# A two-layer graph transformer on one core: the lookups of layer 1's late neighbours done in one run ahead of the edge stage's products, weights moved to SP's queue, last table pieces over fewer slots, and another order of riding chunks

## The chip, the cores and the metric

The kernel runs on one core of a Trainium2 chip. The metric is the device time of one execution in microseconds, the median of several runs. A core has five engines that run at the same time, each with its own stream of instructions: TensorE (PE, matmuls), VectorE (DVE), ScalarE (ACT), GpSimd (POOL) and SyncE (SP). ACT, POOL and SP also issue DMA transfers, each through a queue of its own.

## What is computed

There are 6250 nodes with 128 features, 100000 edges sorted by destination, 16 node types, 32 edge types and 8 heads of 16. One layer of the reference, with the node types' matrices picked by type:

```python
k = typed_linear(x, ntype, Wk); q = typed_linear(x, ntype, Wq); v = typed_linear(x, ntype, Wv)
kT = einsum('nhd,htdo->nhto', k, Watt)          # every node for every edge type
vT = einsum('nhd,htdo->nhto', v, Wmsg)
a = einsum('ehd,ehd->eh', kT[src, :, etype], q[dst]) * pri[:, etype].T / SQRT_D
msg = vT[src, :, etype] * edge_softmax(a, dst)[:, :, None]
hag = segment_sum(msg, dst)
h = silu(typed_linear(hag, ntype, Wa))
h = h * alpha + x * (1 - alpha)                  # alpha = sigmoid(skip[ntype])
x = layernorm(h) * g + b
```

Two such layers follow each other, then `h @ ff_w + ff_b`, and the result is layernorm(input + that).

## The kernel before

**Table and gathers.** Each layer has a table in device memory with one row of 1 KB (K and V, 256 floats) for each pair of a node and an edge type. A put (L1085 in layer 0, L1915 in layer 1, both POOL) writes the rows of 128 nodes for 16 of the edge types, 2 MB; a layer has 98 puts. Destinations are sorted by their number of edges and laid out in blocks of 128, one to a partition, three or four blocks to a superblock. For each edge slot of a block POOL gathers 128 rows of the table with one instruction (L1691, `kv<-tab,ell`) into one column of a ring of 50 columns (`SLOTS`); `ell` holds the row numbers.

**Stages.** First the preparation and layer 0's table: PE, ACT and DVE make the rows, and a ranking of the nodes runs beside it on DVE (`rank_order`). Then `edges()` goes through "visits": fourteen superblocks of layer 0, two "early" visits of layer 1, then layer 1's fourteen. A visit's blocks each take: the products of gathered K with the query (L1707), their reductions (L1712), and a generator `finished()` that makes the softmax (exponentials on ACT at L1492 and L1502), V times weight (L1518), its sums (L1529, L1534). The steps of one block's `finished()` are taken between the products of the next; a ring column is free again when its L1518 is done. After the last block of a superblock `nodes()` makes the new node rows (L1741 `rd`, L1748 `hag`, the typed matrix, the layernorm), and in layer 0 `table()` makes from them the superblock's part of layer 1's table (`kvT` L1870, PE L316, copies into one of three `st` buffers at L323 on ACT and L321 on DVE, put at L1915).

**Pace.** Generators for queries, node rows and table pieces are advanced by `tick`, so many steps for each edge slot (`spread(of, gen, steps, slots)`). POOL's instructions keep the order in which the program writes them. On the other engines a list scheduler sets the order when the kernel is built.

**Lookups.** The two early visits of layer 1 may only read rows of the table that are written early. Their 32 + 44 gathers use lists `ells`, in which slots with late sources are sorted behind. To know which sources are late, `looked()` splits node numbers into row and column, transposes them, writes them to `looks` in device memory (L1282) and reads them back spread over all partitions (L1302), compares them (L1326, `is_equal`), multiplies with a table of late nodes on PE (L1328), compares again (L1333), and turns the flags back with 86 small matmuls and 42 ACT copies (L1319). Its scratch is the third part of `wkqv`, so layer 1's `Wq` is loaded there only afterwards. A sort (tile `key`, MAX and MATCH_REPLACE) then makes `ells` and `negs`. The whole is one generator of 27 steps over 62 slots (`LOOK`), and `table()` runs what is left of the lookups before layer 1's first piece (`while not done`).

**Weights.** Layer 1's `Wk`, `Wv` and its edge weights (`load_edge_weights`, for each head `bdk`, `bdv`, `prit`, L245 to L248) are issued on ACT's queue at the start of the edge stage, ahead of visit 0's query.

**Riders.** In some blocks the last slots are filled in only a few partitions. Such slots "ride" in spare lanes of another slot's gather and are copied into place by SP (L1687, `kv<-kv`). A block with riders is cut into a lead chunk, a bundle with the riders, and a rest.

## Time and profile before

| | before |
|---|---|
| median of 3 runs | 2951.08 us (2948.94 to 2956.63) |
| profiled execution | 2950.59 us, span 2948.7 us |
| granted TensorE clock, mean | 0.652 |
| POOL | 1983.6 us busy (67%), 2118 instructions |
| DVE | 1828.0 us (62%), 4117 |
| PE | 1778.6 us (60%), 5415 |
| ACT | 1108.4 us (38%), 2580 |
| first gather of layer 0 | at 605.2 us |
| first put of layer 1's table | at 752.2 us |
| first gather of layer 1's rest | at 1938.2 us |

A row of a timeline has the start, the duration, the engine, the source line, the operation and what it writes and reads; brackets hold the idle time of the engine just before and what ended it. An engine name with a q (SPq, ACTq) is an issue of a DMA. A row of windows has, after the window and its length, busy time and count for PE, PEld, DVE, ACT and POOL, the granted clock, the DMA engines' share and GB/s. A row of groups has line, engine, operation, tiles, count, busy time, mean time of one in ns, and the idle time before them by releaser.

### The profile page before, as it was taken

What the parts mean: (1) busy time and instruction counts of PE and PEld (TensorE: products, weight loads), DVE (VectorE), ACT (ScalarE), POOL (GpSimd) and SP (SyncE); (2) the same over time, 40 slices, a digit from 0 to 9 for tenths busy, and PEclk for the clock granted to TensorE, in tenths of its full rate; (3) what the DMA queues carried; (4) which work ended last, traced back from release to release, by engine and by line L of the source; (5) the groups of instructions that cost most, each with busy time, mean ns of one, the idle gap of its engine ahead of it and who ended that gap; (6) DMA issues with size and microseconds to landing.
All of it is one profiled execution on the core that took longest, in us unless ns stands there. A gap on an engine that the chain in (4) does not pass through costs nothing. (4 is left out here: it accounts for less than half of the span.)

```text
span 2948.7 us, 22842 instructions
## 1 busy us (share of the span) xinstructions
PE 1778.6 (60%) x5415; PEld 763.8 (26%) x5415; DVE 1828.0 (62%) x4117; ACT 1108.4 (38%) x2580; POOL 1983.6 (67%) x2118
## 2 busy tenths in 40 slices
PE   5999999724676888887587887701433323313121
PEld 2445444411222243232133222200211212101010
DVE  8358323228866777666586655746887767666663
ACT  4876655501423423344243455412332222222220
POOL 5323665566677677777777765767777767777776
PEclk9979766655766656567577566555656656655555
DMA  7998999986667767787787888873333323333331
GB/s 230 403 395 358 385 399 406 396 223 183 217 214 270 272 228 239 266 302 252 257 297 246 287 331 327 306 223 104 105 106 104 107 86 105 106 105 105 106 101 51
DMA packets 186105, 678.28 MB, mean 230 GB/s; under 512 B 55586, under 2 KB 101328, under 8 KB 160912
## 3 DMA queue, kind: packets, MB, share of 16 engines
q0 software_dynamic: 113248, 636.05, 60.8%
q1 hardware_dynamic: 56852, 34.57, 4.3%
q10 hardware_dynamic: 15856, 6.06, 1.0%
q8 instruction: 46, 0.75, 0.1%
q14 instruction: 103, 0.84, 0.1%
HBM read 254.44 MB, written 421.89 MB: 229 GB/s over the span
## 5 line engine op out<-in xcount | busy, mean ns | idle before, releaser
L1691 POOL DMA_INDIRECT kv<-tab,ell x1454 | 1389.2, 955 | 508.5 <-issue 372.6
L323 ACT COPY st<-tb 128x512 f32<-128x512 f32 (+1 forms) x1052 | 717.1, 754 | 540.4 <-PE tb L316 356.2
L1707 DVE TENSOR_TENSOR kv<-kv,tb 128x768 f32<-128x768 f32 (+6 forms) x278 | 262.0, 946 | 534.2 <-DMA kv<-tab,ell 352.8
L292 PE MATMUL nb<-xm,weights 128*128 128x384 f32 (+2 forms) x640 | 368.9, 728 | 351.1 <-DVE xm L275 349.6
L316 PE MATMUL tb<-bdv,kvT 32*128 32x512 f32 x784 | 305.5, 935 | 102.7 <-ACT st L323 99.8
L316 PE MATMUL tb<-bdk,kvT 32*128 32x512 f32 x784 | 294.4, 941 | 35.7 <-ACT st L323 27.7
L316 PE MATMUL tb<-bdv,vT 32*128 32x512 f32 x784 | 290.4, 821 | 33.3 <-ACT st L323 27.5
L292 PEld LDWEIGHTS nb<-xm,weights 128*128 128x128 f32 x640 | 158.8, 269 | 570.9 <-DVE xm L275 359.7
L1712 DVE TENSOR_REDUCE a<-kv 128x48 f32<-128x768 f32 (+6 forms) x278 | 260.0, 939 | 0.7
L1085 POOL DMA_INDIRECT tab<-st,rows x98 | 101.2, 1033 | 199.0 <-ACT st L323 163.0
L1529 DVE TENSOR_TENSOR tb<-kv,tb 128x512 f32<-128x512 f32 (+6 forms) x412 | 228.1, 554 | 2.5
L316 PE MATMUL tb<-bdk,kT 32*128 32x512 f32 x784 | 221.3, 835 | 1.2 <-DVE st L321 0.6
L321 DVE COPY st<-tb 128x512 f32<-128x512 f32 (+1 forms) x124 | 94.1, 759 | 189.7 <-PE tb L316 111.8
L1691 POOL DMA_INDIRECT kv<-tab,ells x166 | 158.9, 957 | 66.9 <-issue 45.9
L1518 DVE TENSOR_TENSOR kv<-kv,tb 128x768 f32<-128x768 f32 (+10 forms) x258 | 192.3, 763 | 0.8
L300 PE MATMUL nb<-ident,hag 128*128 128x128 f32 x98 | 25.9, 406 | 275.5 <-DVE hag L1748 275.5
L275 DVE SCALAR_TENSOR_TENSOR xm<-ntb,nb 128x512 f32<-128x512 bf16 (+2 forms) x224 | 126.7, 593 | 48.1 <-PE nb L300 39.3
L1492 ACT ACTIVATE tb<-a,m 128x17 f32<-128x17 f32 (+12 forms) x328 | 95.3, 290 | 161.9 <-DVE m L1485 153.4
L316 PEld LDWEIGHTS tb<-bdv,vT 32*128 32x128 f32 x784 | 115.0, 230 | 129.8 <-ACT st L323 104.0
L316 PEld LDWEIGHTS tb<-bdv,kvT 32*128 32x128 f32 x784 | 83.5, 255 | 244.4 <-ACT st L323 199.5
L1915 POOL DMA_INDIRECT tab<-st,row x98 | 100.8, 1029 | 67.1 <-ACT st L323 32.7
L316 PEld LDWEIGHTS tb<-bdk,kvT 32*128 32x128 f32 x784 | 80.6, 257 | 181.8 <-ACT st L323 133.9
(395 smaller groups left out, 2274.3 us busy)
## 6 DMA issues: line engine op xcount, KB each, us to landing
kv<-tab,ell POOLq DMA_INDIRECT x1454
weights<-looks SPq DMA_DIRECT2D x40, 128.0 KB
hr<-xrd SPq DMA_DIRECT2D x16, 256.0 KB
kv<-tab,ells POOLq DMA_INDIRECT x166
xrd<-xr POOLq DMA_DIRECT2D x10, 256.0 KB
weights<-looks SPq DMA_DIRECT2D x40, 64.0 KB
hrd<-hs SPq DMA_DIRECT2D x8, 256.0 KB
hr<-xrd SPq DMA_DIRECT2D x10, 192.0 KB
```

The source lines that it names most:

```text
L275: nc.vector.scalar_tensor_tensor(xm[:, :n], ntb[:, :n], float(t), hT[:, :n], op0=ALU.is_equal, op1=ALU.mult)
L292: nc.tensor.matmul(ps[:, :n], w[:, t, :], xm[:, :n], start=(t == types[0]), stop=(t == types[-1]))
L316: nc.tensor.matmul(pt[:, b], yT[s, i * P:(i + 1) * P], bd[s, tt, :], start=True, stop=True)
L323: nc.scalar.copy(to, pt)
L1085: put = nc.gpsimd.indirect_dma_start(out=tabs[0].rearrange("(n t) c -> n (t c)", t=16), out_offset=bass.IndirectOffsetOnAxis(ap=rows1[:, t ...
L1492: nc.scalar.activation(w[:, :, h], av[:, :, h], AF.Exp, scale=-1.0, bias=m[:, h:h + 1], accum_out=den[:, i, h:h + 1])
L1518: nc.vector.tensor_tensor((v_[:, k0:k1] if j or k0 else acc[:, :k1]) .rearrange("p k (h d) -> p k h d", h=H), v_[:, k0:k1].rearrange("p k ...
L1529: nc.vector.tensor_tensor(to, v_, to, op=ALU.add)
L1691: get = nc.gpsimd.indirect_dma_start(out=to.bitcast(I32) if l else to, out_offset=None, in_=tabs[l][:], in_offset=bass.IndirectOffsetOnAxi ...
L1707: nc.vector.tensor_tensor(kk, kk, q[:lanes].unsqueeze(1).to_broadcast([lanes, c, D]), op=ALU.mult)
L1712: nc.vector.tensor_reduce(a[:lanes, j0:j1, :], kk.rearrange("p k (h d) -> p k h d", h=H), axis=AX.X, op=ALU.add)
L1915: put = nc.gpsimd.indirect_dma_start(out=tabs[1].rearrange("(n t) c -> n (t c)", t=16), out_offset=bass.IndirectOffsetOnAxis(ap=row2[:, tg ...
```

## The change

Six things are changed. The lines of the changed kernel are 4 to 70 higher (L1691 becomes L1749, L1707 L1770, L1518 L1576, L1915 L1983, L323 L327).

1. Splitting, transposing and writing the node numbers to `looks` moves into `rank_order`, so into the preparation.
2. `lookups()` replaces the first part of `looked()`. It is run as a whole between the third step of visit 0's query and the rest of it. Loads come in six groups of up to four steps into the three `st` buffers, 128x4x1024 in one transfer; one comparison covers 128x1024; the flags of all 22 steps are summed in one PSUM bank of 44 rows by matmuls with shifted columns of `rowsum`, then copied once (ACT, 44x512), transposed four times and copied to `flags` in four pieces.
3. Layer 1's `Wk`, `Wv`, `Wq` and the 24 loads of edge weights are issued on SP, behind the lookups' loads.
4. The sort is a generator of its own, one step every 11 slots (`SORT`); the wait for the lookups in `table()` is gone.
5. The pieces of layer 0's last visit are spread over 0.62 of the slots in place of 1.0.
6. A bundle with riders is brought into the ring in its old place, but multiplied after the other chunks, and its chunks come last in `finished()` as well.

```diff
-LOOK = 62.0
+SORT = 11.0
+DEEP = 4
...
-    def load_typed(to, w):
-        nc.scalar.dma_start(to, w.rearrange("t d o -> d t o"))
+    def load_typed(to, w, queue=nc.scalar):
+        queue.dma_start(to, w.rearrange("t d o -> d t o"))
...
+                def load(g):
+                    if g >= len(groups):
+                        return
+                    e, n0_, n1_ = groups[g]
+                    st = ep.tile([P, 16, 2 * D], F32, name="st", bufs=STB)
...
+                            nc.sync.dma_start(to, of.unsqueeze(0).to_broadcast(list(to.shape)))
...
+                for g in range(STB):
+                    load(g)
+                sums_ps, turn_ = pairs[0][:R, 0], 0
+                for g, (e, n0_, n1_) in enumerate(groups):
+                    for n in range(n0_, n1_):
...
+                            nc.vector.tensor_scalar(now[:, :2], now[:, :2], rowk, None,
+                                                    op0=ALU.is_equal)
...
+                                nc.tensor.matmul(pt[HALF * h:HALF * (h + 1), :w[h]],
+                                                 lates[:, e, :], now[:, h, :w[h]],
+                                                 start=True, stop=True)
...
+                            nc.vector.scalar_tensor_tensor(
+                                now[:r, 3, a:b], now[:r, 2, a:b], halves[:r],
+                                pt[:r, a:b], op0=ALU.is_equal, op1=ALU.mult)
...
+                            nc.tensor.matmul(sums_ps[:, a:b], rowsum[:r, at:at + R],
+                                             now[:r, 3, a:b], start=(e == n == 0), stop=final)
+                        yield
+                    load(g + STB)
...
-            for _ in queries0(got.setdefault(0, []), *visits[0][1]):
+            asking = queries0(got.setdefault(0, []), *visits[0][1])
+            for _ in range(3):
+                next(asking)
+            for _ in lookups():
+                pass
+            for i, w in enumerate((Wk, Wv, Wq)):
+                load_typed(wkqv[:, i], w[1], nc.sync)
+            load_edge_weights(1, queue=nc.sync)
+            for _ in asking:
                 pass
...
-            done = []
-            spread(extra, looked(), 27, LOOK)
+            spread(extra, sorted_slots(), 1.0, SORT)
...
-                    while not done:
-                        next(extra[0][0])
                     tables[v] = gen
                     spread(pieces, gen, 8 * visits[v][1][1] + 4,
-                           (1.0 if v + 4 < n0 else 0.5 if v + 2 < n0 else 1.0) *
+                           (1.0 if v + 4 < n0 else 0.5 if v + 2 < n0 else
+                            1.0 if v + 1 < n0 else 0.62) *
                            slots(min(v + 2, first1 - 1)))
...
-                    for bundle in bundles:
-                        for (j0, j1, lanes), kv in zip(bundle, [bring(*c[:2]) for c in bundle]):
+                    later = [b for b in bundles[:-1] if riding and len(b) > 1]
+                    for bundle in bundles + later:
+                        if id(bundle) not in brought:
+                            brought[id(bundle)] = [bring(*c[:2]) for c in bundle]
+                            if any(bundle is b for b in later):
+                                continue
+                        for (j0, j1, lanes), kv in zip(bundle, brought[id(bundle)]):
...
-                for i, w in enumerate((Wk, Wv) if fast else (Wk, Wv, Wq)):
-                    load_typed(wkqv[:, i], w[1])
-                load_edge_weights(1)
                 if fast:
                     edges()
                     break
```

How the change moves instructions is seen at three places. The first is SP's queue at the start of the edge stage, in the changed kernel; `ntb` and `hr` are the node types and rows that a visit's query and `nodes()` need, the first pair is visit 0's, the pair at the end visit 1's.

```order
L1179 DMA ntb<-typed 128x384
L1187 DMA hr<-xrd 128x3x128
L1318 DMA st<-looks 128x4x1024
L1318 DMA st<-looks 64x4x512 x2
...
L240 DMA weights<-in_L_gnn_Wq_dram 128x16x128
L249 DMA bdk<-in_L_gnn_Watt_dram 16x32x16
L250 DMA bdv<-in_L_gnn_Wmsg_dram 16x32x16
L252 DMA prit<-in_L_gnn_pri_dram 16x32
...
L1179 DMA ntb<-typed 128x384
L1187 DMA hr<-xrd 128x3x128
```

Before, visit 1's `ntb` stood third on SP, ahead of all lookups, and no weight of layer 1 was on SP; now all lookup loads, three typed weights and 24 small loads are ahead of it.

The second place is DVE where visit 1's first product stands (L1770 here, the fourth block of the program), in the changed kernel; the rows ahead of these are the whole sort.

```order
L1418 TENSOR_REDUCE bad<-key 128x1
L1431 TENSOR_TENSOR ells<-ells,key 128x9
L257 TENSOR_SCALAR prit<-prit 128x32
L1435 TENSOR_REDUCE worst<-bad 128x1
L258 TENSOR_TENSOR bdk<-bdk,prit 128x1024
L279 SCALAR_TENSOR_TENSOR xm<-ntb,nb 128x384 x4
L279 SCALAR_TENSOR_TENSOR xm<-ntb,nb 128x512
L1770 TENSOR_TENSOR kv<-kv,tb_5829 128x6x128
```

Before, the scaling of `bdk` stood ahead of the first product of visit 0, and the sort was spread over the visits behind the first put:

```order
L1326 TENSOR_SCALAR weights<-weights,rowk 128x512 x4
L253 TENSOR_SCALAR prit<-prit 128x32
L254 TENSOR_TENSOR bdk<-bdk,prit 128x1024
L1707 TENSOR_TENSOR kv<-kv,tb_5808 128x6x128
```

So visit 0's products now come among the lookups, and the sort and the scaling come between visit 0 and visit 1.

The third place is POOL's order at the end of layer 0; `tab_64` is layer 1's table, `ells` the early gathers, and the last row is layer 1's rest. Before:

```order
L1691 DMA kv<-tab_64,ells 128x256 x20
L1915 DMA tab_64<-st,row_83 12544x4096
L1691 DMA kv<-tab_64,ells 128x256 x7
L1915 DMA tab_64<-st,row_83 12544x4096
L1691 DMA kv<-tab_64,ells 128x256 x5
L1915 DMA tab_64<-st,row_83 12544x4096
L1691 DMA kv<-tab_64,ells 128x256 x6
L1915 DMA tab_64<-st,row_83 12544x4096
L1691 DMA kv<-tab_64,ells 128x256 x4
...
L1691 DMA kv<-tab_64,ells 128x256 x90
```

Now:

```order
L1749 DMA kv<-tab_64,ells 128x256 x20
L1983 DMA tab_64<-st,row_83 12544x4096 x2
L1749 DMA kv<-tab_64,ells 128x256 x7
L1983 DMA tab_64<-st,row_83 12544x4096 x3
L1749 DMA kv<-tab_64,ells 128x256 x5
L1983 DMA tab_64<-st,row_83 12544x4096
L1749 DMA kv<-tab_64,ells 128x256 x6
L1983 DMA tab_64<-st,row_83 12544x4096 x2
L1749 DMA kv<-tab_64,ells 128x256 x109
```

The eight last puts now stand among the first 38 early gathers, and 19 early gathers stand between the last put and the 90 of the rest (109 in all).

POOL's first 96 gathers and the puts behind them keep their order up to the thirteenth put. Further on there are a few places of the kind that the row of 1327.9 us comes from: there, two puts stood behind eight gathers, and eight more gathers and a third put followed; now all three puts stand behind all sixteen gathers.

204 lines of the change are left out of this document (117 added, 87 removed).

## The prediction

> **What bounds the kernel now.** I read the page's busy times first, then its slices by time, then the POOL engine's own timeline.
>
> ```profile
> PE 1778.6 (60%) x5415; PEld 763.8 (26%) x5415; DVE 1828.0 (62%) x4117; ACT 1108.4 (38%) x2580; POOL 1983.6 (67%) x2118
> ...
> POOL 5323665566677677777777765767777767777776
> ...
> L1691 POOL DMA_INDIRECT kv<-tab,ell x1454 | 1389.2, 955 | 508.5 <-issue 372.6
> ```
>
> No engine looks full, but 372.6 of the gathers' idle time is "issue": POOL waited for nothing. A stretch without other work shows what that means (columns: window, length, then busy time and count of PE, PEld, DVE, ACT, POOL, clock, DMA share, GB/s):
>
> ```profile
> 0.00:605.00 605.00, 513.55 (x2110) 258.50 (x2110) 277.22 (x679) 370.65 (x725) 286.01 (x351) 0.78 0.94 371
> 605.00:752.00 147.00, 63.44 (x235) 27.25 (x235) 97.03 (x248) 19.46 (x79) 93.27 (x96) 0.62 0.70 176
> 2400.00:2500.00 100.00, 28.96 (x77) 16.67 (x77) 70.75 (x140) 26.82 (x117) 75.65 (x80) 0.60 0.36 105
> ```
>
> 80 gathers in 100 us: one every 1.25 us (0.95 and 0.30 of issue) is POOL's full pace, reported as 76% busy. POOL works strictly in program order, so from the first gather on the time is its count of instructions at 1.25 us plus its real waits. Ahead of 605 the DMA share is 0.94 at 371 GB/s: layer 0's table is written at the transfers' pace. The waits that the change can reach are these rows of POOL (start, duration, instruction, in brackets the idle time before and its releaser):
>
> ```profile
> 605.21 1.00 POOL L1691 DMA_INDIRECT kv<-tab,ell  x1 [18.77 <-DMA tab<-st,rows]
> ...
> 719.41 0.94 POOL L1691 DMA_INDIRECT kv<-tab,ell  x1 [4.27 <-DVE tb L1518]
> ...
> 752.18 1.02 POOL L1915 DMA_INDIRECT tab<-st,row  x1 [13.83 <-ACT st L323]
> 981.14 0.94 POOL L1691 DMA_INDIRECT kv<-tab,ell  x1 [7.88 <-DVE bn L1777]
> 1327.89 0.99 POOL L1915 DMA_INDIRECT tab<-st,row  x1 [5.72 <-ACT st L323]
> 1925.37 1.01 POOL L1915 DMA_INDIRECT tab<-st,row  x1 [0.30 <-ACT tb L1492]
> 1938.21 0.97 POOL L1691 DMA_INDIRECT kv<-tab,ells  x1 [11.84 <-DMA tab<-st,row]
> 2377.72 0.94 POOL L1691 DMA_INDIRECT kv<-tab,ell  x1 [13.86 <-DVE t L1765]
> ```
>
> From the first gather at 605.2 to the first put of layer 1's table stand 96 gathers, 120 us at full pace, so that put could go at 725.2. It goes at 752.2. These 27 us are the largest sum in reach.
>
> **Term 1, lookups and first put.** Why the put is late is seen on ACT, DVE and SP:
>
> ```profile
> 609.50 4.06 ACTq L245 DMA_DIRECT2D bdk<-in_L_gnn_Watt_dram  x1
> ...
> 622.47 0.35 ACTq L248 DMA_DIRECT2D prit<-in_L_gnn_pri_dram  x1
> ...
> 630.60 0.50 ACTq L248 DMA_DIRECT2D prit<-in_L_gnn_pri_dram  x1
> ...
> 644.76 0.33 ACTq L248 DMA_DIRECT2D prit<-in_L_gnn_pri_dram  x1
> 645.50 0.48 ACT L1167 COPY qT<-nb 128x384 f32<-128x384 f32 x1 [37.62 <-DMA kv<-tab,ell]
> 622.57 0.42 DVE L1280 CAST lookb<-tb 83x256 bf16<-83x256 f32 x1 [10.72 <-DMA looks<-lookb]
> ...
> 649.67 0.94 DVE L1707 TENSOR_TENSOR kv<-kv,tb 128x768 f32<-128x768 f32 x1
> 709.42 0.30 DVE L1741 RECIPROCAL rd<-den 128x24 f32<-128x24 f32 x1
> ```
>
> ACT stands from 607.9 to 645.1 issuing the edge weights; visit 0's query copy is behind them, and DVE's first product comes at 649.7, 44 us after the first gather. The put's chain then runs from L1741 at 709.4 to 752.2, 42.8 us. In it and before it DVE does the lookups:
>
> ```profile
> L1333 DVE SCALAR_TENSOR_TENSOR weights<-weights,halves,tb 128x512 bf16<-128x512 bf16 (+1 forms) x22 | 16.1, 731 | 12.5 <-issue 5.8 <-PE tb L1328 3.2 <-DMA weights<-looks 3.1
> L1326 DVE TENSOR_SCALAR weights<-weights,rowk 128x512 bf16<-128x512 bf16 (+1 forms) x42 | 14.2, 354 | 13.0 <-DMA weights<-looks 13.0
> L1707 DVE TENSOR_TENSOR kv<-kv,tb 128x768 f32<-128x768 f32 (+3 forms) x13 | 12.5, 965 | 0.6 <-ACT tb L1471 0.6
> ```
>
> In the changed order ACT has no loads ahead, so products start with the lookups. The lookups load 8.16 MB as before (by the code), now in six groups. DVE's leg to the resume (its first product of visit 1): group 0 lands about 613, an estimate from 1.5 MB at some 300 GB/s beside the gathers; 22 L1333 at 0.731 = 16.1; 20 comparisons of twice the width, not shown in this trace: each between 0.354 (only a fixed cost) and 0.708 (two narrow ones), I take 0.6, nearer the doubled row, 12 in all (7 to 14); six products and six reductions of visit 0 at 0.965, 11.6, and their softmax sums, about 8. That makes 613 + 48 = 661. Then the sort, which now stands whole ahead of the resume:
>
> ```profile
> 752.00:960.00 208.00, 21.30 (x151) 0.66 0.71 244
> 737.00:752.00 15.00, 3.23 (x23) 0.84 0.37 104
> ```
>
> These windows, of the tile `key` alone, hold 24.5 us; with the few small operations on `ells` and `negs` I take 28. So DVE reaches 689 without idle time. SP is the other leg: its last lookup group goes about 640, when the third buffer's first steps are through; three typed weights, 3.1 MB, are 8 us at the 371 GB/s ahead of 605; then eight heads of edge weights. ACT's rows have seven heads from 622.5 to 644.8, 3.2 us each, so eight take 25 and `prit` and visit 1's rows are there about 675 to 680. DVE's leg is the later one, and the resume comes at 688. From it to L1741 are some 14 us of DVE work (bdk scaling, eight xm, two products, sums), and then at most the old 42.8 less the lookup work within it, which I put at 39: the first put at **741**, 11 us sooner. Bounds: 725 (POOL's own pace, -27) and 765 (rival A, +13). If the ring keeps POOL a little before that, it costs nothing, as long as 96 gathers are through by 741.
>
> The Trainium skill (SBUF — State Buffer, "SBUF: two separate sides") speaks against lookups packed together: it says that while DVE runs an operation that takes both ports, GpSimd can't write its descriptors. The 96 POOL instructions above, with 42 fast comparisons beside them, took 93.27/96 = 0.97 us against 0.955 over all, so this trace shows hardly any of it. By the rule, 12 us of comparisons would move POOL's own pace from 725 to 737, still ahead of the 741 that I take; the sum stays, only its lower bound falls away.
>
> The nodes' transposes and the write to `looks`, moved ahead of 605, are some 2.5 us of DVE (shifts, a cast, two copies like the 0.42 of L1280) that lie beside table scatters at a DMA share of 0.94; if the cover were gone they would cost that. The removed 84 loads, tiny matmuls and flag copies lie off POOL's path: worth nothing beyond the times above.
>
> **Term 2, order of the riding bundles.** The K=41 block of layer 0:
>
> ```profile
> 955.73 1.22 DVE L1707 TENSOR_TENSOR kv<-kv,tb 128x1024 f32<-128x1024 f32 x1 [16.25 <-DMA kv<-kv]
> ...
> 980.20 0.68 DVE L1518 TENSOR_TENSOR tb<-kv,a 128x512 f32<-128x512 f32 x1
> ```
>
> POOL's wait at 981.1 ends with the lead chunk's L1518 at 980.2, which frees its ring columns. With other chunks multiplied while the riders (SP copies) are on the way, the scores (L1479, 970.4) come about 2.7 us sooner, but one more L1518 of about 0.9 now stands ahead: -2 (0 to -4). The like wait at 2377.7 has four xm in that place; I take 0 (bounds -3 and +3).
>
> **Term 3, 1327.9.** Two puts in a row wait 5.7 there for `st`. In the new order eight more gathers stand ahead of them (10 us of POOL), so `st` has time; the sum takes -3, since POOL meets its next puts sooner (0 to -5.4).
>
> **Term 4, last pieces at 0.62.** The eight last puts and then layer 1's rest:
>
> ```profile
> 1880.00:1900.00 20.00, 16.98 (x43) 4.88 (x41) 13.91 (x18) 10.19 (x33) 15.12 (x17) 0.50 0.90 339
> 1900.00:1920.00 20.00, 12.99 (x36) 4.27 (x36) 17.22 (x26) 8.80 (x24) 15.43 (x16) 0.50 0.97 356
> L321 DVE COPY st<-tb x16: 1214/1220/1225, 1860.8 to 1917.7; 128x1024 f32<-128x1024 f32 x16
> ```
>
> Before, the last put is issued at 1925.4 and its 2 MB land 12.8 us later. Now 19 of the early gathers stand behind it, 23.8 us, which cover that landing. But the put must come early for that: PE is busy 17 of 20 us at a granted clock of 0.50, and DVE's half of the copies, two for each `st`, go from 1860.8 to 1917.7: 57 us for eight, some 7 each. If `st` keeps its old times (the eighth at about 1919), the rest starts at 1919 + 23.8 = 1942.8, +4.6; with pieces made denser by a few us, 1938. The other bound is DMA: 8 x 2.1 MB and 18 gathers of 0.13 MB at 356 GB/s are 54 us from 1869, so about 1925 to 1930, -9. I take **+2**, nearer the rows of PE (bounds -9 and +6).
>
> **Sum.** -11 - 2 - 3 + 2 = -14, on the profiled execution's own 2950.6 us, of which 2948.7 is span and 1.9 lies around it; the median of the three runs is 2951.1, 0.5 above. So 2936.6 + 0.5, **2937 us**. Layer 1's stretch after 1938, POOL at full pace on 645 gathers, moves as a block.
>
> **Rivals.**
>
> A, slower: SP's queue takes over ACT's wait. The 27 weight loads stand on SP ahead of visit 1's `ntb` and `hr`, and those feed the queries and ACT's `hb`, behind which the later copies wait. If a head takes 8 us, as the second did on ACT (622.5 to 630.6), eight take 64: 640 + 8 + 64 = 712, first put 765, +13, and with the other terms +10: 2961. SP's leg is the later one from 5 us a head on, and from 6.7 the kernel is slower than before. For it: pieces of 64 bytes (16x32x16 floats) at a DMA share of 0.92, below, and 37 us on ACT. Against: the last six heads took 14 us, 2.4 each.
> ```profile
> 605.00:652.00 47.00, 9.71 (x31) 5.52 (x31) 12.57 (x37) 2.51 (x10) 35.64 (x37) 0.57 0.92 198
> ```
> The Trainium skill (DMA: Bandwidth & Descriptors, "Specifications") gives 512 bytes as the least for line rate, which the share of 0.92 at 198 GB/s, half of the 400 ahead of 605, agrees with.
>
> B, no change: the put comes sooner, but what is gained is given back, at 1327.9, at 981 or at the rest's start (+6), because the pieces behind it are set by PE and not by POOL: -11 + 6 + 2 = -3, 2948.
>
> C, faster: the 11.84 wait goes in full: -9 instead of +2, 2926.
>
> D: the change doesn't do what it says, the sort and the comparisons (not the loads) hold DVE until 700: first put 753, +1; with the other terms -2, 2949.
>
> **How the numbers follow.** Forecast 0.48, A 0.16, B 0.15, C 0.10, D 0.11. A measurement of this kernel tells 0.3%, 8.9 us, from no change. Faster: most of the forecast (0.44) and all of C, 0.55 with a little of D. Slower: A and a part of B where the puts wait more, 0.18. The rest, 0.27, same. The forecast's own range is 2926 to 2946; with A's lower part and B above and C below it is **2920 to 2960**.
>
> **What would show it.** First put (L1983, the changed kernel's line) at 735 to 748 with a wait under 15; the first product of visit 1 near 688, released by DVE's own sort and not by `prit` or `hr`. Term 2: the wait at 981 at about 6. Term 4: no wait on the table's transfer ahead of the rest, but one on `st` at the puts before it. I am wrong if visit 1's rows land after 700 on SP, or if the edge stage starts later than 605.

## The result, and the profile after

| | before | after |
|---|---|---|
| median of 6 runs | 2950.01 us (2942.89 to 2956.63) | 2974.38 us (2966.53 to 2981.65) |
| ratio, 95% interval | | 1.008 [1.0055, 1.0104] |
| span of the profiled execution | 2948.7 us | 2971.0 us |
| first gather of layer 0 | 605.2 | 602.4 |
| first put of layer 1's table | 752.2 | 758.6 |
| first gather of layer 1's rest | 1938.2 | 1958.3 |

The kernel became 0.8% slower, 22.3 us in the profiled executions, where 14 us less were forecast. On the page after, PE, DVE, ACT and POOL are all busy about as long as before or less; the time went into waits:

```profile
PE 1758.2 (59%) x5355; PEld 754.1 (25%) x5355; DVE 1833.3 (62%) x4103; ACT 1101.6 (37%) x2537; POOL 1982.2 (67%) x2118
...
L1749 POOL DMA_INDIRECT kv<-tab,ell x1454 | 1389.5, 956 | 523.7 <-issue 376.2
```

The gathers still take 956 ns and their "issue" is still 0.3 us each; the idle time ahead of them grew from 508.5 to 523.7. Since POOL has the same 1620 gathers in both kernels, the two timelines of POOL can be laid over each other: the start of the n-th gather after, less that of the n-th before, says where time was lost. This table is worked out from them.

| gather number | before, us | after, us | difference | what lies between it and the line above |
|---|---|---|---|---|
| 0 | 605.2 | 602.4 | -2.8 | preparation |
| 96 | 753.5 | 759.9 | +6.4 | up to the first put |
| 245 | 960.9 | 966.4 | +5.4 | |
| 280 | 1018.3 | 1029.7 | +11.3 | the first riders (981 before) |
| 480 | 1297.0 | 1308.9 | +12.0 | |
| 500 | 1333.0 | 1336.6 | +3.6 | the two puts at 1327.9 before |
| 520 | 1365.7 | 1378.5 | +12.9 | |
| 600 | 1475.6 | 1488.6 | +13.0 | |
| 700 | 1616.6 | 1632.9 | +16.2 | |
| 836 | 1854.2 | 1869.9 | +15.7 | |
| 885 | 1938.2 | 1958.3 | +20.1 | the last pieces |
| 1200 | 2334.9 | 2354.2 | +19.2 | |
| 1240 | 2399.0 | 2423.5 | +24.5 | layer 1's riders |
| 1619 | 2876.8 | 2899.1 | +22.3 | |

So the loss has four places: +9.2 from the first gather to the first put, some +10 in the middle of layer 0 (+5.9 to gather 280, +0.9 from 480 to 520, +3.2 from 600 to 700), +4.4 at the last pieces and +5.3 at the riders of layer 1. The rows of POOL in the timeline after, at these places:

```profile
602.41 1.00 POOL L1749 DMA_INDIRECT kv<-tab,ell  x1 [16.77 <-DMA ell<-ell]
...
718.33 0.94 POOL L1749 DMA_INDIRECT kv<-tab,ell  x1 [22.48 <-DVE tb L1576]
758.62 1.02 POOL L1983 DMA_INDIRECT tab<-st,row  x1 [12.99 <-ACT st L327]
977.40 1.10 POOL L1983 DMA_INDIRECT tab<-st,row  x1 [3.77 <-ACT st L327]
981.75 1.51 POOL L1749 DMA_INDIRECT kv<-tab,ell  x1 [3.24 <-DMA tab<-st,row]
990.13 0.95 POOL L1749 DMA_INDIRECT kv<-tab,ell  x1 [4.37 <-DVE tb L1576]
1004.35 0.94 POOL L1749 DMA_INDIRECT kv<-tab,ell  x1 [3.09 <-DVE tb L1587]
1345.76 0.97 POOL L1983 DMA_INDIRECT tab<-st,row  x1 [0.55 <-ACT st L327]
1356.20 0.94 POOL L1749 DMA_INDIRECT kv<-tab,ell  x1 [1.82 <-DMA tab<-st,row]
1362.77 1.02 POOL L1983 DMA_INDIRECT tab<-st,row  x1 [5.63 <-DMA kv<-tab,ell]
1377.15 1.08 POOL L1749 DMA_INDIRECT kv<-tab,ell  x1 [3.21 <-DVE hs L1898]
1904.29 0.99 POOL L1983 DMA_INDIRECT tab<-st,row  x1 [3.63 <-DVE tb L1587]
1911.07 0.97 POOL L1983 DMA_INDIRECT tab<-st,row  x1 [5.78 <-ACT st L327]
1943.29 0.94 POOL L1749 DMA_INDIRECT kv<-tab,ells  x1 [1.76 <-DMA tab<-st,row]
2397.01 0.99 POOL L1749 DMA_INDIRECT kv<-tab,ell  x1 [14.38 <-DVE t L1833]
2411.76 0.94 POOL L1749 DMA_INDIRECT kv<-tab,ell  x1 [5.01 <-DVE t L1833]
```

Two of the old waits went as meant: the 11.84 us ahead of layer 1's rest (1.76 is left) and the 5.72 at 1327.89 (0.55). The old 7.88 at 981 has become four waits, 14.5 us in all, and behind 2397 stands a second wait of 5.01 that before does not have.

**The head.** From the first gather to the first put it is 156.2 us after and 147.0 before. What DVE did in that time, first in windows (columns as before), then in the groups of that stretch:

```profile
602.00:669.00 67.00, 29.42 (x82) 10.25 (x82) 39.88 (x76) 2.34 (x6) 50.75 (x53) 0.53 1.00 260
669.00:706.00 37.00, 0.92 (x4) 0.50 (x3) 34.51 (x263) 1.51 (x5) 20.45 (x22) 0.50 0.72 155
```

```profile
L1357 DVE SCALAR_TENSOR_TENSOR st<-st,halves,tb 128x512 bf16<-128x512 bf16 (+1 forms) x22 | 15.6, 731 | 7.2 <-DMA st<-looks 6.2 <-PE tb L1350 0.8
...
L1341 DVE TENSOR_SCALAR st<-st,rowk 128x1024 bf16<-128x1024 bf16 x20 | 9.0, 501 | 15.7 <-DMA st<-looks 15.7
```

During the lookups the DMA share is 1.00 and DVE is busy for 39.9 of 67 us: it waits 21.9 us (15.7 and 6.2) for the loads of `looks`. In the 37 us after them it is full, with the sort. The rows of its timeline from there to the first put's chain:

```profile
669.06 0.24 DVE L1377 COPY flags<-tb 128x80 f32<-128x80 f32 x1 [0.20 <-PE tb L1374]
...
704.96 0.18 DVE L257 TENSOR_SCALAR prit<-prit 128x32 f32<-128x32 f32 x1 [0.21 <-issue]
...
713.70 0.69 DVE L279 SCALAR_TENSOR_TENSOR xm<-ntb,nb 128x512 f32<-128x512 bf16 x1 [5.44 <-PE nb L304]
714.30 0.95 DVE L1770 TENSOR_TENSOR kv<-kv,tb 128x768 f32<-128x768 f32 x1
...
721.82 0.29 DVE L1809 RECIPROCAL rd<-den 128x24 f32<-128x24 f32 x1
```

Lookups until 669.3, sort until 704.7, then the scaling of `bdk`, the `xm` and a wait of 5.44 for PE, visit 1's first product at 714.3, `rd` at 721.8, and the put 36.8 later. SP's issues of the weights and visit 1's rows (timeline of SP):

```profile
653.71 0.77 SPq L240 DMA_DIRECT2D weights<-in_L_gnn_Wk_dram  x1
...
665.99 4.92 SPq L249 DMA_DIRECT2D bdk<-in_L_gnn_Watt_dram  x1
...
688.01 0.48 SPq L252 DMA_DIRECT2D prit<-in_L_gnn_pri_dram  x1
688.73 0.35 SPq L1179 DMA_DIRECT2D ntb<-typed  x1
```

Eight heads go out in 22.5 us (666.0 to 688.5), 2.8 each. The rows of visit 1 are behind them at 689, still ahead of the end of the sort.

### The profile page after: what moved, and what is told of

Same layout as the page of the kernel before. It is cut to its first block, busy times and chain, and to the rows that moved or that the text cites. A ratio compares the mean times of both kernels' runs of the same rounds, so it can differ in the third digit from the quotient of the medians.

```text
span 2971.0 us, 22452 instructions
## 1 busy us (share of the span) xinstructions
PE 1758.2 (59%) x5355; PEld 754.1 (25%) x5355; DVE 1833.3 (62%) x4103; ACT 1101.6 (37%) x2537; POOL 1982.2 (67%) x2118
## 5 line engine op out<-in xcount | busy, mean ns | idle before, releaser
L1749 POOL DMA_INDIRECT kv<-tab,ell x1454 | 1389.5, 956 | 523.7 <-issue 376.2
L327 ACT COPY st<-tb 128x512 f32<-128x512 f32 (+1 forms) x1052 | 716.8, 754 | 546.9 <-PE tb L320 348.5
L1770 DVE TENSOR_TENSOR kv<-kv,tb 128x768 f32<-128x768 f32 (+9 forms) x278 | 262.0, 946 | 548.3 <-DMA kv<-tab,ell 394.3
L320 PE MATMUL tb<-bdv,kvT 32*128 32x512 f32 x784 | 296.4, 900 | 121.3 <-ACT st L327 115.9
L320 PE MATMUL tb<-bdk,kvT 32*128 32x512 f32 x784 | 285.2, 903 | 51.1 <-ACT st L327 40.5
L1775 DVE TENSOR_REDUCE a<-kv 128x48 f32<-128x768 f32 (+9 forms) x278 | 259.8, 939 | 0.9
L1587 DVE TENSOR_TENSOR tb<-kv,tb 128x512 f32<-128x512 f32 (+7 forms) x412 | 227.9, 553 | 2.7
L1749 POOL DMA_INDIRECT kv<-tab,ells x166 | 158.6, 956 | 57.3 <-issue 44.1
L1576 DVE TENSOR_TENSOR kv<-kv,tb 128x768 f32<-128x768 f32 (+11 forms) x258 | 192.4, 763 | 0.8
L279 DVE SCALAR_TENSOR_TENSOR xm<-ntb,nb 128x512 f32<-128x512 bf16 (+2 forms) x224 | 126.5, 593 | 64.5 <-PE nb L304 50.6
L1983 POOL DMA_INDIRECT tab<-st,row x98 | 100.0, 1020 | 85.2 <-ACT st L327 38.6
```

The lines of the kernel that those rows point to most:

```text
L279: nc.vector.scalar_tensor_tensor(xm[:, :n], ntb[:, :n], float(t), hT[:, :n], op0=ALU.is_equal, op1=ALU.mult)
L320: nc.tensor.matmul(pt[:, b], yT[s, i * P:(i + 1) * P], bd[s, tt, :], start=True, stop=True)
L327: nc.scalar.copy(to, pt)
L1576: nc.vector.tensor_tensor((v_[:, k0:k1] if j or k0 else acc[:, :k1]) .rearrange("p k (h d) -> p k h d", h=H), v_[:, k0:k1].rearrange("p k ...
L1587: nc.vector.tensor_tensor(to, v_, to, op=ALU.add)
L1749: get = nc.gpsimd.indirect_dma_start(out=to.bitcast(I32) if l else to, out_offset=None, in_=tabs[l][:], in_offset=bass.IndirectOffsetOnAxi ...
```

## The experiments

The texts on record name theories by letters. Q is that the order on SP makes the first put late: with visit 1's rows behind the weights, the scheduler has nothing else for DVE and puts the whole sort ahead of visit 1. Its rival, W, is that the lookups as one dense run do it, in whatever order SP works. R is that the riders' new order costs, in POOL's order and in layer 1. P is that the pieces at 0.62 cost by themselves.

All these runs fell on other chips than the first comparison, and on those the kernel before takes 3429 to 3468 us in place of 2950 (the last section). Ratios are to the kernel before on the same chip. "Put" is the time from the first gather to the first put.

### One part undone at a time

Rows first: the weights go out on SP behind visit 1's rows.

```diff
-            for i, w in enumerate((Wk, Wv, Wq)):
-                load_typed(wkqv[:, i], w[1], nc.sync)
-            load_edge_weights(1, queue=nc.sync)
...
+                    if v == 0:
+                        for _ in range(3):
+                            next(asked)
+                        for i_, w in enumerate((Wk, Wv, Wq)):
+                            load_typed(wkqv[:, i_], w[1], nc.sync)
+                        load_edge_weights(1, queue=nc.sync)
```

> The changed kernel with one edit: layer 1's typed and edge weights are issued on SP behind visit 1's node types and rows, no longer ahead of them; nothing is left out. Theory Q (the order on SP): in the changed kernel visit 1's rows stood behind 27 weight loads, so the whole sort, 35 us from 669.5 to 704.6, came ahead of visit 1's query and products; with the rows first the sort falls apart over the visits, the first put goes from 758.6 to 738 to 745 and the wait of 22.5 us at 718 goes to under 8; the time falls by 10 to 18 us. Rival W (the amount of DVE work, whatever its order): lookups and loads keep DVE until 669 and the put stays later than 753; the time falls by less than 5 us.

Riders in the old order:

```diff
-                    later = [b for b in bundles[:-1] if riding and len(b) > 1]
+                    later = []
```

> The changed kernel with one edit undone: bundles with riders are multiplied in their place and finished in their place, as before; nothing is left out. Theory R (freed last): in the K=41 block of layer 1 the riders' columns come next in the ring behind the lead's but are finished last, which adds the wait of 5.0 us at 2411.8 and takes nothing from the one of 14.4 at 2397; undone, the second wait goes and the time falls by about 5 us from that block, and by 0 to 5 from the like block at 980 to 1005. Rival: the new order is worth the 2 us I forecast in layer 0 and nothing in layer 1; undone, the time rises by 2 us or stays.

The last pieces over all slots again:

```diff
-                            1.0 if v + 1 < n0 else 0.62) *
+                            1.0) *
```

> The changed kernel with one edit undone: the pieces of layer 0's last visit over 1.0 of the slots in place of 0.62; nothing is left out. Theory P (PE-bound pieces): the eight last puts then wait for nothing and the 12 us wait on the last put's landing is back; the stretch from the 855th gather to the rest's first one is 4 to 5 us shorter, so the time falls by 4 to 5 us. Rival: 0.62 covers the landing as meant and the losses at the puts are there for another reason (the late start of the stage); undone, the time rises by 2 to 8 us.

The weights on ACT's queue, ahead of visit 0's query, as before:

```diff
+            for i, w in enumerate((Wk, Wv, Wq)):
+                load_typed(wkqv[:, i], w[1])
+            load_edge_weights(1)
...
-            for i, w in enumerate((Wk, Wv, Wq)):
-                load_typed(wkqv[:, i], w[1], nc.sync)
-            load_edge_weights(1, queue=nc.sync)
```

> The changed kernel with one edit undone: layer 1's weights are issued on ACT's queue at the start of the edge stage, as before (its Wq too); nothing is left out. Theory Q: visit 1's rows are again near the front of SP, so the sort is spread over the visits; but ACT again stands on its issues for about 35 us, so visit 0's products start about 645, behind the lookups, and the first put goes at 745 to 755: the time falls by 4 to 13 us. Rival W: the lookups run whole are the cause, the put stays at 755 to 765 and the time within 4 us.

The first three once more on another chip, with a fourth kernel that puts rows first and undoes riders and pieces too:

> The same kernel as in the run with visit 1's rows ahead of the weights on SP, on another chip (on the first one the kernel before took 3468 us, so that small waits drown there; even so the put came 184 us after the first gather, against 201 and 202 in the two kernels that keep the changed order on SP). Theory Q: on a chip where the kernel before takes 2950, the first put is 138 to 145 us after the first gather (changed kernel 156.2, before 147.0), and the time 10 to 18 us under the changed kernel's 2974. Rival W: put over 150 us after the first gather, time over 2969.

> The same kernel as in the run with the riders' old order, on another chip. Theory R: in layer 1's K=41 block one wait of about 14 us is left where the changed kernel has 14.4 and 5.0; time 2965 to 2970. Rival: waits of the same sum within 2 us, time 2974 or more.

> The same kernel as in the run with the last pieces over all slots, on another chip. Theory P: from the 836th gather to the 885th 83.5 to 85 us as before (changed kernel 88.4), one wait of 12 us on the put's landing in it; time 2968 to 2971. Rival: that stretch is as long as in the changed kernel, time 2974 or more.

> The changed kernel with three edits: weights behind visit 1's rows on SP, riders in the old order, last pieces over all slots; nothing is left out. If Q, R and P hold and the three places are independent, their gains add: 2974 less 15, 5 and 4 is 2950, and less than the kernel before where the put is sooner than its 147 us: 2940 to 2950. If the puts behind the first one give the gain back (at 977 to 1004 and 1356 to 1377 in the changed kernel), 2955 to 2965.

| | ratio [95%] | put |
|---|---|---|
| rows first | 1.0002 [0.9969, 1.0035]; again 1.0049 [1.0024, 1.0075] | 182.4; 187.1 |
| riders old | 1.0071 [1.0037, 1.0105]; again 1.0136 [1.0086, 1.0187] | 200.7; 199.5 |
| pieces full | 1.0006 [0.9975, 1.0037]; again 1.0040 [1.0010, 1.0071] | 199.9; 200.4 |
| weights on ACT | 0.9940 [0.9911, 0.9968] | 181.1 |
| rows first, riders old, pieces full | 1.0057 [1.0018, 1.0096] | 182.1 |

What follows: the kernels that leave the head alone have their put at 200; the ones that take the weights from ahead of visit 1's rows have it at 181 to 187. The order on SP does set a part of the put there, as Q says. The other part is work that only changes its place: with rows first, DVE comes to `rd` 123 to 126 us after the first gather, in the kernels that leave the head alone at 153 to 157, so some 30 us sooner; but the sort then stands behind it, and the put is only 8 to 18 us sooner. The times don't follow the put cleanly, and undoing the riders' order makes the kernel longer, where R, taken for the time, would make it shorter; the second wait in layer 1 does go, as R says. Undoing the pieces alone gains nothing that can be measured, against P.

### The change again, and ACT's queue

> The changed kernel itself, nothing edited and nothing left out, as the yardstick for the runs on the chips where the kernel before takes about 3450. If the loss of 24 us is of the same kind there, its ratio to the kernel before is 1.006 to 1.012, and the two runs with visit 1's rows ahead (1.000 and 1.005) and with full pieces (1.001 and 1.004) lie under it; if the ratio is under 1.003, the loss belongs to the chips of the first comparison and the runs on the others tell nothing of it.

> The changed kernel with three edits undone: weights on ACT's queue at the start, riders in the old order, last pieces over all slots; lookups still whole and their flags still in one bank; nothing is left out. Theory Q with R and P: what is left of the change is then no loss; ratio to the kernel before 0.990 to 1.000 (the run with the weights alone on ACT had 0.994). Rival W: the whole run of lookups costs by itself; ratio over 1.004.

> The changed kernel with the weights on ACT's queue at the start, a second time on another chip, beside the changed kernel itself. Theory Q: 10 us or more faster than the changed kernel beside it, first put 12 to 20 us sooner after the first gather. Rival W: within 5 us of it.

The first is the changed kernel itself. The second has the weights on ACT with riders and pieces undone. The third is the kernel of weights on ACT run again, with the new riders' order in it.

| | ratio [95%] | put |
|---|---|---|
| the change itself | 1.0055 [1.0032, 1.0079] | 196.4 |
| weights on ACT, riders old, pieces full | 1.0043 [1.0016, 1.0071] | 179.5 |
| weights on ACT again | 1.0027 [1.0000, 1.0055] | 183.0 |

The change is slower on this chip too, by about the same share. With the weights on ACT the put comes 13 us sooner and the median is 12.0 us shorter (3443.62 against 3455.61, same chip), yet still not below the kernel before. In the profiled executions nothing of the 13 us is left at the end: from the first gather to the last it is 2756.0 us in both. And the second kernel, which has of the change only the dense lookups, the sort and the moved preparation (and `Wq` with the other weights), is at 1.0043, over the 1.004 that its text gives as the sign of W. Rows first and the change itself, on two chips, differ by 9.3 at the first put, by 4.4 at the 42nd (906.7 against 902.3) and by -1.0 at the 44th (924.8 against 925.8): what is won at the first put need not arrive.

### Parts alone

Riders alone, on the kernel before (the sixth part of the change and nothing else); the head alone (the changed kernel with `later = []` and the factor 1.0); the pieces alone on the kernel before; rows first with full pieces:

> The kernel before with one part of the change alone: bundles with riders multiplied and finished last; nothing is left out. Theory R: in the two K=41 blocks a second wait comes behind the first, since the riders' columns are next in the ring and freed last; 5 us more in layer 1's block, 0 to 5 in layer 0's: ratio 1.001 to 1.004, and the second wait seen in POOL's rows. Rival, as forecast: layer 0's wait at 981 falls by 2 us, layer 1's stays: ratio 0.999 to 1.000.

> The changed kernel with two edits undone: riders in the old order, last pieces over all slots; so lookups, weights on SP and sort are what is left of the change; nothing is left out. If the head of the edge stage is the main loss (first put 9 us later after the first gather), the ratio to the kernel before is that of the changed kernel, 1.006 to 1.010 on a chip where that takes 2950, with layer 1's single wait of 13 to 14 us; if riders and pieces are, it is 1.002 to 1.004.

> The kernel before with the riders' new order alone, a second time. Theory R: seven puts of layer 0 stand behind 4 to 13 more gathers and layer 1's K=41 block has two waits, about 14 and 5 us; on a chip where the kernel before takes 2950 the ratio is 1.003 to 1.006. Where it takes 3450 it was 0.997: there puts wait for st anyway, so that later puts cost nothing. Rival: under 1.000 on any chip.

> The kernel before with the last pieces over 0.62 of the slots alone; nothing is left out. Theory P: the stretch from the ninth put from the end to layer 1's rest is 5 us longer than the kernel before's 96.5 on a chip where that takes 2950, ratio 1.001 to 1.003; where it takes 3450 that stretch was 111 to 116 with either value, ratio 0.998 to 1.002. Rival: the stretch is shorter and the ratio under 0.998.

> The changed kernel with two edits: weights behind visit 1's rows on SP, last pieces over all slots; riders stay in the new order; nothing is left out. Theory Q: first put 180 to 187 us after the first gather where the kernel before takes 3450 (changed kernel 196 to 201), 138 to 147 where it takes 2950 (156); ratio to the kernel before 0.5% under the changed kernel's if POOL sets the pace behind the put, the same if table pieces do.

| | ratio [95%] | put |
|---|---|---|
| riders alone | 0.9967 [0.9942, 0.9992]; again 0.9968 [0.9935, 1.0002] | 169.4; 170.2 |
| head alone | 1.0094 [1.0052, 1.0136] | 196.5 |
| pieces alone | 1.0024 [0.9989, 1.0059] | 171.5 |
| rows first, pieces full | 1.0054 [1.0015, 1.0092] | 188.8 |

What follows: **of the parts run alone, only the head makes the kernel longer on these chips.** It does so by 0.9%, and its put comes 25 to 27 us later than in the three runs with the old head. How much of that is the head's own is less sure: in the profiled executions its first gather comes at 613.6, against 599.7 and 599.9 for the two old heads on that chip, so 14 us of the difference between those executions lie ahead of the edge stage. Nor is it shown that the late put makes the late end. The change and riders alone ran on one chip; in their profiled executions the change is 27.0 us later at the first put (196.4 against 169.4) and 30.1 at the end (3450.7 against 3420.6). But weights on ACT ran there too, with a put only 13.6 us later than riders alone, and from the first gather to the last it is 30.3 us longer all the same. Timelines of POOL, the change on that chip and then the kernel before with riders alone:

```profile
608.62 1.01 POOL L1749 DMA_INDIRECT kv<-tab,ell  x1 [18.62 <-DMA ell<-ell]
...
805.02 1.01 POOL L1983 DMA_INDIRECT tab<-st,row  x1 [19.59 <-ACT st L327]
...
2793.93 0.95 POOL L1749 DMA_INDIRECT kv<-tab,ell  x1 [5.04 <-DVE t L1833]
```

```profile
608.88 1.00 POOL L1692 DMA_INDIRECT kv<-tab,ell  x1 [18.66 <-DMA tab<-st,rows]
...
778.25 1.02 POOL L1926 DMA_INDIRECT tab<-st,row  x1 [14.71 <-ACT st L323]
...
2767.64 0.94 POOL L1692 DMA_INDIRECT kv<-tab,ell  x1 [5.05 <-DVE t L1776]
```

The wait of 5 us in layer 1 stands in both, and in every kernel here with the riders' new order; none with the old order has it. In layer 0's block of 41 slots the same second wait stands at gather 262: 3.09 us in the change on the first chip (the row at 1004.35), 2.2 to 4.8 in every other kernel with the new order, and none with the old one. The riders' order also moves POOL's own order. The number of gathers ahead of a put, counted in the traces, is the same for before, and the head alone; and the same for the change, and riders alone:

| put | 13 | 14 | 20 | 42 | 43 | 56 | 57 |
|---|---|---|---|---|---|---|---|
| old riders' order | 232 | 239 | 281 | 497 | 497 | 619 | 623 |
| new riders' order | 245 | 245 | 289 | 505 | 505 | 627 | 627 |

Seven puts stand behind 4 to 13 more gathers, through that edit alone. On these chips no loss by this can be measured, and riders alone even gain 0.3%. That the puts wait for their `st` there all along, so that a later place takes no time from them, fits; where a gain comes from stays open (counted from the first gather, riders alone is 20 us ahead of pieces alone, on the same chip, at the ninth-last put). The wait for `st` is seen in the view of waits (total, times, longest), first of the kernel before on the first chip, then of riders alone on a later one:

```profile
POOL tab L1915 <- ACT st L323: 32.7, 11, 13.8
```

```profile
POOL tab L1926 <- ACT st L323: 249.7, 37, 15.6
```

On the first chip the puts wait 33 us in all, and POOL's rows lose time behind three of these places, each time where two or three puts now follow each other: +5.9 behind puts 13 and 14 (gathers 245 to 280), +9.3 behind puts 42 and 43 (500 to 520), +3.2 behind puts 56 and 57 (600 to 700); at put 20 nothing is lost. That the edit causes these three is argued from the coincidence of places; riders alone were not run on that chip.

The pieces at 0.62 can't be told from 1.0 on the later chips: the stretch from the ninth-last put to layer 1's rest is 111 to 116 us with either.

### Equal issue of the weights

To separate the dense lookups from the place where the weights go out, both heads got the same one: on SP, head by head, spread over 20 slots of visit 0 behind visit 1's rows. In one kernel on the old lookups (with riders' new order), in the other on the changed kernel (with full pieces):

```diff
+            def next_weights():
+                for h in range(H):
+                    load_edge_weights(1, [h], nc.sync)
+                    yield
...
+                    if v == 0:
+                        next(asked)
+                        spread(more, weighing[0], 10, 20.0)
```

> The kernel before with two edits: riders in the new order, and layer 1's edge weights, Wk and Wv issued on SP head by head behind visit 1's rows, between the lookups' loads, no longer on ACT; lookups and sort as before; nothing is left out. Theory Q carried further (what the put waits for is where the weights are issued): ACT is free for visit 0's query, products begin 20 us or more sooner than in the kernel before, the first put comes 150 to 165 us after the first gather (170 in the two kernels with the old head on such chips), and the ratio falls under the 0.997 of the riders alone by what the put gains, to 0.990 to 0.995. Rival: loads on SP, mixed with the lookups', hold those back; put at 170 or later, ratio 0.997 or more.

> The changed kernel with two edits: the weights are issued on SP head by head behind visit 1's rows (edge weights first, then Wk, Wv, Wq), last pieces over all slots; riders in the new order, lookups whole; nothing is left out. Theory Q: put as with the rows first, 180 to 188 us after the first gather, ratio 1.000 to 1.005, and 0.5% or more over the kernel before with the same spread weights: what is left is the price of lookups and sort ahead. Rival: the whole lookups cost nothing once the weights are out of the way, put 170 or sooner and ratio under 0.998.

Ratios 1.0007 [0.9985, 1.0030] and 1.0009 [0.9987, 1.0032], puts 185.3 and 182.9. The rows of POOL, old lookups and then dense ones:

```profile
600.43 1.00 POOL L1708 DMA_INDIRECT kv<-tab,ell  x1 [15.70 <-DMA tab<-st,rows]
...
785.75 1.02 POOL L1944 DMA_INDIRECT tab<-st,row  x1 [30.04 <-ACT st L323]
```

```profile
603.29 1.01 POOL L1762 DMA_INDIRECT kv<-tab,ell  x1 [18.68 <-DMA ell<-ell]
...
786.14 1.02 POOL L1998 DMA_INDIRECT tab<-st,row  x1 [33.09 <-ACT st L327]
```

With the weights on SP, spread like this, dense and spread lookups come out alike; in the first run the rival's figures came (put 170 or later, 0.997 or more), and in the second the 0.5% between the two kernels did not. With the weights on ACT they do not come out alike: there the dense lookups have the put 8 to 14 us later, and their time is 0.4 and 0.6% longer in two comparisons on one chip (1.0043 against the kernel before; 1.0027, with the new riders and pieces, against 0.9967 of riders alone), though not in the run that gave 0.994. DVE's rows say why the puts differ; all times are from the first gather, the comparison is the start of the last one at L1333 or its like:

| | first product | `rd` of visit 0 | last comparison | put |
|---|---|---|---|---|
| before, first chip | 44.5 | 104.2 | 128.8 | 147.0 |
| riders alone | 50.5 | 127.0 | 150.3 | 169.4 |
| riders alone again | 51.4 | 126.5 | 152.0 | 170.2 |
| pieces alone | 51.1 | 126.8 | 152.3 | 171.5 |
| old lookups, weights spread on SP | 11.1 | 93.2 | 167.6 | 185.3 |
| dense lookups, weights on ACT again | 92.0 | 141.5 | 88.2 | 183.0 |
| dense lookups, weights spread on SP | 17.8 | 124.2 | 87.4 | 182.9 |

In all five runs with the old lookups the put stands 17.7 to 19.2 us behind the last comparison, wherever `rd` is. Taking the weights from ACT did bring visit 0 forward, by 33 us at `rd`; but the lookups ended 15 to 17 us later, and the put with them. So what the old put waits for, by these rows, is the end of the lookups, which the program runs to their end ahead of layer 1's first piece; why they took longer in that run is not shown. With dense lookups the put is led by visit 0 and the sort instead. With the weights on ACT, visit 0's query copy stands behind their issue there, and beside the dense loads, with `Wq` as a third typed weight, the copy comes 79 to 82 us after the first gather, in place of 42 to 43. ACT's rows, dense lookups with weights on ACT again and then riders alone, whose first gathers are at 601.98 and 608.88:

```profile
683.76 0.48 ACT L1193 COPY qT<-nb 128x384 f32<-128x384 f32 x1 [76.57 <-DMA ntb<-typed]
```

```profile
651.29 0.48 ACT L1167 COPY qT<-nb 128x384 f32<-128x384 f32 x1 [39.72 <-DMA kv<-tab,ell]
```

So neither the dense lookups nor the place of the weights costs by itself in every company; each decides how long the other takes. The spread of the time of dense lookups with weights on ACT, 0.994 and 1.0027 in two runs of one kernel, stays open.

None of these kernels was run on the first chip, so none is shown to beat the one before there, and the causes named for the first chip rest on its two traces. On the later ones the best is the kernel before with the riders' new order alone, 0.997 twice.

## Why the prediction was wrong

**Term 1, the first put: forecast 741 (-11), measured 758.6 (+6.4).** This is the step that failed most. Its leg on DVE ended the lookups at 661 and the sort 28 us later, with the resume put down as 688; measured are 669.3 and 704.7, 16.7 us after that. All of it is the sentence that DVE reaches the sort's end "without idle time", a term put at nothing: DVE waited 21.9 us for the loads of `looks`, at a DMA share of 1.00 and 260 GB/s, where I had taken 300. The rows of before that stand in the prediction already had 13.0 and 3.1 us of waiting for these loads. The work itself was sized rather high: 76 us of it from 613 to 689 in the prediction, 69.0 us busy out of 91.9 in these windows of DVE, so 22.9 us of idle time:

```profile
613.00:669.30 56.30, 35.73 (x65) 0.53 1.06 276
669.30:704.90 35.60, 33.23 (x259) 0.50 0.74 159
```

The sort took 35.4 us in place of 28 because some 9 us of visit 0's products and sums, which the prediction had counted ahead of it, ran among it. Its own operations were sized well, `key` 23.0 us by this window, 24.5 before; the comparisons were 0.50 us each, below the 0.6 taken.

```profile
602.00:759.00 157.00, 22.97 (x177) 0.59 0.68 171
```

From the sort's end to `rd` it was 17.1 in place of 14, with 5.4 of it a wait for PE, which in turn could start only behind the `xm`. From `rd` to the put it was 36.8 for 39. That is 16.7 + 3.1 - 2.2 = 17.6, the whole miss of the term.

Rival D came nearest in its numbers, DVE held until 700 and the put at 753, but by another way: it named the sort and the comparisons, and not the loads, and it is the loads that DVE waited for. Rival A's condition did not come true on the first chip: a head took 2.8 us against the 5 at which SP would be the later leg, and visit 1's rows went out 16 us before the sort's end. On the later chips, though, moving the weights behind these rows brought the put 8 to 18 us forward. A named the place, SP's queue, but not the way: the scheduler's order for DVE changes with it. On these chips the kernels with the changed head have the sort done 136 to 140 us after the first gather; with rows first it falls apart over the visits and is still going on at the put.

The premise of the term, that ACT's 37 us of issuing weights made the old put late, is half right by the run of the old lookups with weights on SP. ACT's wait did make visit 0 late there; but the put follows the end of the lookups, 18 us behind it on the first chip as on the others.

The 12 us that the prediction allows for comparisons holding up POOL came to 1: of the gathers in the 67 us of dense lookups, the 15 that run beside a comparison took 1.02 us in the mean and the others 0.95. POOL waits 22.48 us for the ring behind them anyway, so it costs nothing.

**Term 2, riders: forecast -2, measured +5.9 at gathers 245 to 280 and +5.3 in layer 1.** The sign was wrong. In layer 1 the runs show the cause: a second wait of 5.0 us in every kernel with the new order. I had looked at when the riders' scores come. But a chunk that is multiplied last is also finished last, and gives its ring columns back last, while POOL goes round the ring in the old order and wants those columns right behind the lead chunk's. DVE's rows show it (timeline of DVE after): the V product of the bundle's own slots, that of its riders in 35 lanes, and then the sum at L1587 that reads the bundle's first columns. The product at L1576 is written in place here, so the columns are free only when that sum is done, at 2411.5, and POOL goes on at 2411.8:

```profile
2407.34 1.21 DVE L1576 TENSOR_TENSOR kv<-kv,tb 128x1024 f32<-128x1024 f32 x1
...
2410.29 0.39 DVE L1576 TENSOR_TENSOR kv<-kv,tb 35x256 f32<-35x256 f32 x1
...
2410.83 0.66 DVE L1587 TENSOR_TENSOR tb<-kv,tb 128x512 f32<-128x512 f32 x1
```

In layer 0 the same second wait is 3.1 of the 14.5 us; 7.0 more are the put's wait of 3.77 and the 3.24 on a table transfer, behind three puts in a row. The gathers that stand ahead of more puts were seen for the pair at 1327.9 only, and there counted as a gain.

**Term 3: forecast -3, measured -8.4 and then +9.3.** The wait of 5.72 did go, for the reason given; the other 2.6 are the two puts themselves, which stand behind gather 500 now. Between gathers 500 and 520 these 2.6 are back, and with them come new waits of 1.82 and 5.63, the first of them on a table transfer, 10 us behind three puts in a row. The wait of 3.21 that follows is not new; before has it ahead of the same gather (timeline of POOL before):

```profile
1364.40 0.94 POOL L1691 DMA_INDIRECT kv<-tab,ell  x1 [3.21 <-DMA tab<-st,row]
```

So the term came to +0.9. Rival B named this place, but its condition, a sooner first put, did not come true.

**Term 4, last pieces: forecast +2, measured +4.4, within its bounds.** The mechanism was right: the wait on the table's transfer is gone, and the puts before wait for `st` instead (3.63 and 5.78 above). If `st` kept its old times, the working gave +4.6; I should have taken that end, since the rows of PE had nothing to make the pieces denser with.

**The sum.** Forecast -14, measured +22.3: of the 36 us between them 17.4 are Term 1, 13.2 Term 2, 3.9 Term 3 and 2.4 Term 4; the stretches between, with the +3.2 behind puts 56 and 57 that no term had, come to -0.7.

## What to carry to other kernels

A stretch of work that is made dense runs at the pace of its slowest supplier: before counting its instructions back to back, divide its bytes by the rate at which that stretch is fed, and carry over the waits that the old rows already show. List whatever else stands on its engine between its end and what waits for it. When a piece of work is moved on one engine, look at the fixed orders that hang on it (here POOL's puts behind more gathers, and the ring's columns in the old order), not only at the wait that it is to remove. A wait that is long (ACT's 37 us) is not yet the one that binds: in the run that took it away, visit 0 was done 33 us sooner and the put came no sooner, because the lookups ended no sooner.

## What was not expected of the hardware

The same program has two very different times. The changed kernel takes 2971.0 us of span on the chip of the first comparison and 3450.7 on a later one, and the kernel before 2950 and 3429 to 3468. The first gather comes at 602 and 609, so the preparation takes as long, and a gather still takes 0.95 us. From there on ACT, DVE and PE stand still without a releaser on their own core: the view of waits has, for the change on the later chip,

```profile
ACT st L327 <- remote: 235.6, 51, 9.9
POOL tab L1983 <- ACT st L327: 219.8, 34, 19.6
ACT st L327 <- issue: 111.3, 44, 20.2
...
ACT tb L1550 <- remote: 85.6, 37, 3.8
```

and on the first chip

```profile
POOL tab L1983 <- ACT st L327: 38.6, 21, 13.0
...
ACT st L327 <- issue: 2.6, 3, 1.9
```

where no line of ACT is released by "remote". In layer 1, where POOL sets the pace, it does 66 gathers in 100 us in place of 76 (2400 to 2500 of both), in the order of the later chip's row and then the first's:

```profile
2400.00:2500.00 100.00, 47.16 (x101) 22.90 (x101) 70.88 (x185) 25.63 (x113) 62.34 (x66) 0.59 0.29 85
```

```profile
2400.00:2500.00 100.00, 26.44 (x73) 15.88 (x73) 65.56 (x136) 19.42 (x85) 72.18 (x76) 0.55 0.35 100
```

What makes them stand still is open, and so is whether it is the chip or something else that the later runs have in common. It bears on the experiments: this idle time falls differently in each program, so differences of a few tenths of a per cent between two different kernels there can't be laid to one edit by the time alone, and the readings above rest on rows and counts where they can.
